# Layer 2's 3x3 convolution: neighbour columns stacked by ScalarE copies instead of DMAs

## The chip, the cores and the metric

The kernel runs on one NeuronCore of a Trainium2 chip. The metric is the device time of one execution in microseconds (us). The engines are TensorE (PE, with its weight loads PEld), VectorE (DVE), ScalarE (ACT), GpSimd (POOL) and SyncE (SP). DMAs are issued from the queues of SP, POOL and ACT. Each engine works through its own instructions in the order of the program and waits where an operand is not ready or a buffer is not free.

## The reference

Four layers of the form x = x + layer(GN(x)) on x of shape (1024, 16, 16, 16): batch, height h, width w, channels. GN is a group normalisation without weights, 8 groups of two channels. Layer 0 is a tensor-train matrix product, layers 1 and 3 are two steps of a cellular automaton, and layer 2, which the change is about, is a plain convolution:

```python
def _L2_conv_ref(x, filters, bias):
    out = jax.lax.conv_general_dilated(x, filters, window_strides=(1, 1), padding='SAME',
        dimension_numbers=('NHWC', 'HWIO', 'NHWC'))
    return out + bias
...
x = x + _L2_conv_ref(_gn(x), L2_conv_filters, L2_conv_bias)   # filters (3, 3, 16, 16)
```

## The kernel before

The batch is cut into two halves of 512 images, n = 0 and 1. One half of x is held in SBUF at a time for the layer that works (`X0` or `X1`, each 128 partitions x 32 lines x 512 floats, 8 MB), while the other buffer is loaded from DRAM and normalised for the stage that follows. All is float32. Between layers x lies in DRAM (`xf`).

In layer 2 a line holds one image row h and one half of its columns (wh = 0: columns 0 to 7, wh = 1: columns 8 to 15). Its 128 partitions are 4 column pairs x 16 channels x 2 columns of a pair. So a matmul with a 128x128 weight (`fw`, one for each of the three rows of the filter) does all of the filter inside one half of the columns: `inner(h, y)`. What crosses the middle is left: the rightmost column of the left half needs column 8 and the leftmost of the right half needs column 7. `across(h)` adds this with one matmul a half into 32 of the 128 output partitions. Its moving operand is `hx`: for one row h the 16 channels of the neighbour column in the three rows h-1, h, h+1, stacked in 48 partitions (from 0 for wh = 0, from 64 for wh = 1). `halo(k)` fetches it for four rows at a time with DMAs from SBUF to SBUF on SP's queue (`L1153`, `L1156`), three for each half, one more each at the top edge.

Two rows h and h+1 make a group of steps: `first(h)`, `inner(h, 1)`, `first(h+1)`, `inner(h+1, 1)`, then `across` of both, then `last(h)`, `last(h+1)`. Six PSUM banks hold the accumulators `po` of three rows, two for each row. `finish(h)` empties the two banks of row h with ScalarE (bias added, into `r`, six buffers, `L1191`) and adds the result to x in DRAM with an accumulating DMA on GpSimd's queue (`L1192`). `finish` of an even row stands in `last(h)`, that of an odd row in `first` of the next row.

`run(layer, us, loads, (background, lo, hi), by)` weaves three things into one program: the main steps of the layer, the loads of the other half (issued evenly over the first `by` of the steps), and the background steps (the normalisation of the half being loaded), placed by their costs between the fractions `lo` and `hi` of the steps. The normalisation sums the lines on DVE (`s1`, `L589` and `L592`), takes the mean with a matmul (`pmean`), copies it to SBUF on ScalarE (`m`, `L636`), subtracts it (`L621`), squares the lines on ScalarE (`sq`, `L606`) and adds the squares on DVE (`L592`, `s2s` at `L596`), takes the variance with a matmul (`pvar`), and multiplies by the inverse root. In the first half of layer 2 the other half is normalised whole (`norm_lines`, line layout); in the second in four quarters (`norm_cw`, for layer 3's layout, in which spread matmuls `pr` follow). In the second half the loads read what the first half has just accumulated in DRAM. `line_sum(..., own=True)` forms the sum of squares: one step makes the square of the next two lines and adds it. `t4` is the buffer of squares and partial sums, three of them in these stages. `hx` has three buffers.

Of the kernel before, what the change touches and what calls it, by code (L numbers as in the profile page):

```python
# [12 lines left out]
ALU = mybir.AluOpType  # L13
# [5 lines left out]
B, S, C = 1024, 16, 16  # L19
P = 128  # L20
NB = 512
# [82 lines left out]
def conv_preact_kernel(ctx: ExitStack, tc: tile.TileContext, a: dict, out: bass.AP):  # L104
# [55 lines left out]
    def cst(name, shape, dt=F32):  # L160
        return const.tile(shape, dt, tag=name, name=name)
# [245 lines left out]

    b2 = cst("b2", [P, 1])

    convw = cst("convw", [P, 448])  # L410

    def conv_weights():


        room = work([P, 2, NB], "t4", "convn").rearrange("p a b -> p (a b)")
        fn = room[:, 0:384].rearrange("p (y w o) -> p y w o", y=3, w=8)
        hn = room[:, 384:400]
        fw = convw[:, 0:384].rearrange("p (y w o v) -> p y w o v", y=3, w=4, v=2)
        hw = convw[:, 384:448].rearrange("p (e o v) -> p e o v", e=2, v=2)
        V.memset(room[:, 0:400], 0.0)  # L420
        V.memset(hw, 0.0)
        f = a["L2_conv_filters"]
        with nc.allow_non_contiguous_dma(reason="weights"):
            for w in range(8):
                for kw in range(3):
                    if 0 <= w + kw - 1 < 8:
                        wi = w + kw - 1
                        G.dma_start(
                            fn[32 * (wi // 2) + wi % 2 : 32 * (wi // 2) + 32 : 2, :, w],
                            f[:, kw].rearrange("y i o -> i y o"),  # L430
                        )
            for wh in range(2):
                for y in range(3):
                    r0 = 64 * wh + 16 * y
                    G.dma_start(hn[r0 : r0 + 16], f[y, 2 - 2 * wh])
            for m in range(4):
                for v in range(2):
                    G.dma_start(
                        b2[32 * m + v : 32 * m + 32 : 2], a["L2_conv_bias"].unsqueeze(1)
                    )  # L440

        def spread():
            for y in range(3):
                V.tensor_copy(fw[:, y], fn[:, y].rearrange("p (w v) o -> p w o v", v=2))
            for wh in range(2):
                rows = slice(64 * wh, 64 * wh + 64)
                for e in range(2):
                    V.tensor_copy(hw[rows, e, :, 1 - wh], hn[rows])
                V.memset(hw[64 * wh : 64 * wh + 16, 1], 0.0)

        return spread

# [125 lines left out]
    def line_sum(parts, name, own, dear=False):  # L578

        st = {}

        def first():
            if own:
                st["t"] = parts[0]()
                return add(parts[1])()
            st["t"] = work([P, 2, NB], "t4", name)
            V.tensor_tensor(st["t"], parts[0](), parts[1](), ALU.add)  # L589

        def add(p):
            return lambda: V.tensor_tensor(st["t"], st["t"], p(), ALU.add)  # L592

        def last():
            st["s"] = work([P, NB], "s", name + "s")
            V.tensor_tensor(st["s"], st["t"][:, 0], st["t"][:, 1], ALU.add)  # L596

        x = 1.2 if dear else 0.0
        return st, [(1.2 + 2 * x, first)] + [(1.2 + x, add(p)) for p in parts[2:]] + [(0.8, last)]

    def squares(X, l0, n, on_act):
        def piece(l):
# [367 lines left out]
    def layer_train():  # L970
# [160 lines left out]

    conv = dict(
        fw=convw[:, 0:384].rearrange("p (y m) -> p y m", y=3),
        hw=convw[:, 384:448].rearrange("p (e m) -> p e m", e=2),
    )

    def layer_conv(X, n):

        st = {}

        def start():
            halo(0)

        def halo(k):
            t = st["h", k] = work([P, 4, NB], "hx", "hx")
            for wh in range(2):
                src = X[slice(97, 128, 2) if wh else slice(0, 32, 2), 16 * (1 - wh) : 16 * (1 - wh) + 16]
                for y in range(3):  # L1150
                    r0, h0 = 64 * wh + 16 * y, 4 * k + y - 1
                    lo, hi = max(h0, 0), min(h0 + 4, S)
                    nc.sync.dma_start(t[r0 : r0 + 16, lo - h0 : hi - h0], src[:, lo:hi])  # L1153
                    if lo > h0:

                        nc.sync.dma_start(t[r0 : r0 + 16, 0:1], src[:, 0:1])  # L1156

        def inner(h, y):
            for wh in range(2):
                T.matmul(  # L1160
                    st["po", h][wh], conv["fw"][:, y], X[:, 16 * wh + h + y - 1],
                    start=y == max(0, 1 - h), stop=y == min(2, S - h),
                )

        def across(h):
            rows = 32 if h == S - 1 else 48
            for wh in range(2):
                cols = slice(0, 32) if wh else slice(96, 128)
                T.matmul(
                    st["po", h][wh][cols], conv["hw"][64 * wh : 64 * wh + rows, h == 0],  # L1170
                    st["h", h // 4][64 * wh : 64 * wh + rows, h % 4], start=False, stop=False,
                )

        def first(h):
            if h % 2 == 0 and h > 0:
                finish(h - 1)
            if h % 4 == 1 and h + 4 < S:
                halo(h // 4 + 1)
            st["po", h] = [bank([P, NB], "o", "po2") for _ in range(2)]
            inner(h, max(0, 1 - h))  # L1180

        def last(h):
            inner(h, min(2, S - h))
            if h % 2 == 0 or h == S - 1:
                finish(h)

        def finish(h):

            for wh in range(2):
                r = work([P, NB], "r", "conv")  # L1190
                A.activation(r, st["po", h][wh], AF.Identity, bias=b2)  # L1191
                G.dma_start(rows_wc(xf[2][n], wh, h), r.unsqueeze(1), accum_op=ALU.add)  # L1192

        steps = []
        for h in range(0, S, 2):
            for j in (h, h + 1):
                steps.append(lambda j=j: first(j))
                if 0 < j < S - 1:
                    steps.append(lambda j=j: inner(j, 1))
            steps += [  # L1200
                lambda h=h: (across(h), across(h + 1)), lambda h=h: last(h), lambda h=h: last(h + 1)
            ]
        return start, steps

# [313 lines left out]
    last = alone(N, 3) + rstd(nst, slice(96, 128)) + [3] + scaled(N, [3])  # L1518
    nca_sb = dict(t4=2, s=3, n=2, wq=5, mask=1, f=5, hid=8, u=2, r=4, nx=1)
    nca_ps = dict(h=6, o=2)  # L1520
    conv_sb, conv_ps = dict(gn, s=3, r=6, hx=3), dict(o=6, m=2)
    on_vector[0] = True
    with ExitStack() as es:
        shared[0] = "o"
# [8 lines left out]
    with ExitStack() as es:  # L1533
        shared[0] = "m"
        stage(es, conv_sb, conv_ps)
        run(layer_conv(X0, 0), 108, load_wc(X1, xf[2][1]), (norm_lines(X1), 0.09, 1.1), by=0.12)
        run(
            layer_conv(X1, 1), 108, [put(L3)] + load_cw(X0, xf[3][0]), (norm_cw(X0, True), 0.09, 1.04), by=0.12
        )
    with ExitStack() as es:  # L1540
        shared[0] = "o"
# [41 lines left out]
```

## Time and profile before

Median 3199.57 us of three runs (3197.21 to 3203.37). The profiled execution spans 3190.1 us.

| engine | busy us | share of the span |
|---|---|---|
| PE | 3058.5 | 96% |
| DVE | 1785.6 | 56% |
| ACT | 1018.3 | 32% |
| POOL | 670.6 | 21% |

Layer 2 takes the window from 2339.7 to 2591.5 us. In it the groups that matter here are (instructions are records; a float32 matmul leaves two):

| line | engine | what | count | busy us | mean ns |
|---|---|---|---|---|---|
| L1160 | PE | inner matmuls, 128x128 weights | 368 | 168.5 | 609 |
| L1169 | PE | crossing matmuls, 48 (32) x 32 weights | 128 | 35.8 | 646 |
| L1191 | ACT | evictions | 64 | 42.6 | 685 |
| L606 | ACT | squares of two lines | 32 | 32.7 | 1052 |
| L621 | DVE | subtract the mean, multiply | 62 | 72.2 | 1165 |
| L1192 | POOL | accumulating DMAs issued | 64 | 55.5 | 949 |

How to read a profile line of a group: line, engine, operation, out<-in by the program's names, shape and count; then busy time and mean; then the engine's idle time just before these instructions and what ended it. Two matmuls can overlap, so a mean longer than the spacing is usual. "PEclk" is the clock that TensorE was granted, in tenths.

### The profile page before, as it was taken

Reading aid. Unit: us, or ns where it says so; the run is one execution under the profiler, and the core shown is the slowest. Engines: PE = TensorE matmul, PEld = TensorE weight load, DVE = VectorE, ACT = ScalarE, POOL = GpSimd, SP = SyncE. Lnnn points to the kernel's source line nnn. Section 1 sums busy time; section 2 is a strip of 40 time slices with the busy share of each in tenths; the row PEclk is TensorE's granted clock in tenths of the full one; section 3 lists DMA queues with packets and bytes.
Section 4 is the critical chain, followed back from the end, with each engine's and each line's share of the span. In section 5 each row is a group of like instructions: output and inputs, shape, how many; then the busy total and the mean of one; then the engine's idle time right before and its main releaser. Section 6 shows DMA issues by size and latency. Waiting matters only on the chain.

```text
span 3190.1 us, 37179 instructions
## 1 busy us (share of the span) xinstructions
PE 3058.5 (96%) x13874; PEld 1260.3 (40%) x13874; DVE 1785.6 (56%) x2378; ACT 1018.3 (32%) x1690; POOL 670.6 (21%) x706
## 2 busy tenths in 40 slices
PE   7899899999999999999999999999979899999996
PEld 5444333444444444444444433333323233333332
DVE  5255345755554555544556678558757647754222
ACT  4331221100001000000111166666624356655553
POOL 1116532200000000000000034435432124432221
PEclk8999999999999999999999999999989999999998
DMA  7535545443333433322222254454476765433445
GB/s 283 201 142 97 121 101 160 133 144 104 104 109 132 146 116 104 104 98 96 90 95 90 76 168 133 129 167 154 139 192 110 185 139 173 136 92 115 128 137 186
DMA packets 243299, 424.77 MB, mean 133 GB/s; under 512 B 37844, under 2 KB 91952, under 8 KB 239408
## 3 DMA queue, kind: packets, MB, share of 16 engines
q1 hardware_dynamic: 217824, 368.63, 35.5%
q0 software_dynamic: 24480, 53.48, 8.3%
q8 instruction: 110, 1.80, 0.2%
q14 instruction: 69, 0.57, 0.1%
q10 hardware_dynamic: 816, 0.30, 0.0%
HBM read 238.78 MB, written 165.60 MB: 127 GB/s over the span
## 4 chain that ended last, share of the span: by engine, by line
issue 46%; PE 31%; POOL 8%; DMA 4%; DVE 2%; SPq 1%; ACT 1%; POOLq 0%; DVEq 0%; ACTq 0%
PE ph L1410 11%; PE po L1078 10%; PE po L1263 4%; POOL res L1313 4%; POOL u L1312 4%; PE po L1160 2%; DMA xn<-xf 1%; PE L_conv_pe L382 1%; SPq L941 1%; DVE xn L621 1%; DMA hx<-xn 1%; PE pw L1001 1%; PE ptout L948 1%; DVE sq L592 1%; POOL L_conv_wy L394 0%
## 5 line engine op out<-in xcount | busy, mean ns | idle before, releaser
L1078 PE MATMUL po<-xn,w 128*128 128x512 f32 x3584 | 1584.3, 598 | 4.6 <-DVE xn L892 4.6
L1078 PEld LDWEIGHTS po<-xn,w 128*128 128x128 f32 x3584 | 669.9, 190 | 852.6 <-issue 833.7
L1413 ACT ACTIVATE hid<-ph,pack 128x512 f32<-128x512 f32 x1024 | 653.9, 686 | 429.2 <-PE ph L1410 308.4
L1114 DVE TENSOR_TENSOR r<-r,po 128x512 f32<-128x512 f32 x576 | 377.8, 683 | 499.0 <-PE po L1078 476.3
L1312 POOL TENSOR_TENSOR u<-u,mask 128x512 f32<-128x512 f32 x128 | 202.5, 1582 | 1858.9 <-DMA nx<-xn 1241.7
L1410 PE MATMUL ph<-xn,wq 32*128 32x512 f32 x3664 | 573.1, 613 | 1.5 <-DMA wq<-L_conv_wy 1.5
L1006 ACT COPY w<-pw 128x512 f32<-128x512 f32 (+1 forms) x320 | 150.6, 558 | 1194.0 <-issue 970.4
L1410 PEld LDWEIGHTS ph<-xn,wq 32*128 32x128 f32 x3664 | 228.6, 184 | 263.3 <-issue 231.4
L1410 PE MATMUL ph<-xn,pack 32*128 32x512 f32 x1288 | 302.2, 631 | 4.5 <-ACT hid L1413 3.2
L1263 PE MATMUL po<-hid,pack 128*32 128x512 f32 x2048 | 283.0, 609 | 1.2 <-DVE u L1275 0.9
L1019 DVE TENSOR_TENSOR w<-w 128x512 f32<-128x512 f32 x320 | 211.2, 684 | 115.2 <-ACT w L1006 114.7
L621 DVE TENSOR_TENSOR xn<-xn,m 128x1024 f32<-128x1024 f32 x160 | 225.9, 1461 | 47.1 <-ACT m L636 47.1
L1313 POOL TENSOR_TENSOR res<-res,u 128x512 f32<-128x512 f32 x128 | 215.2, 1681 | 17.0 <-PE po L1263 2.7
L1275 DVE SCALAR_TENSOR_TENSOR u<-po,pack,xn 128x512 f32<-128x512 f32 x128 | 95.9, 749 | 157.6 <-PE po L1263 150.9
L1160 PE MATMUL po<-xn,convw 128*128 128x512 f32 x368 | 168.5, 609 | 0.0
L1410 PEld LDWEIGHTS ph<-xn,pack 32*128 32x128 f32 x1288 | 114.5, 187 | 100.7 <-issue 61.7
L1114 DVE TENSOR_TENSOR xn<-xn,po 128x512 f32<-128x512 f32 x96 | 64.3, 684 | 125.9 <-PE po L1078 125.8
L592 DVE TENSOR_TENSOR sq<-sq 128x1024 f32<-128x1024 f32 x78 | 110.6, 1418 | 15.2 <-ACT sq L606 12.0
L1263 PEld LDWEIGHTS po<-hid,pack 128*32 128x32 f32 x2048 | 42.9, 108 | 189.7 <-issue 137.4
L394 POOL DMA_DIRECT2D L_conv_wy<-xn x160 | 89.0, 563 | 99.0 <-ACT xn L152 90.7
L1160 PEld LDWEIGHTS po<-xn,convw 128*128 128x128 f32 x368 | 69.3, 193 | 99.3 <-issue 96.7
L592 DVE TENSOR_TENSOR s<-s,xn 128x1024 f32<-128x1024 f32 x60 | 86.4, 1441 | 29.1 <-DMA xn<-xf 27.9
(163 smaller groups left out, 1776.9 us busy)
## 6 DMA issues: line engine op xcount, KB each, us to landing
xf<-r SPq DMA_DIRECT2D x112, 512.0 KB, 3.8
xn<-xf SPq DMA_DIRECT2D x96, 512.0 KB, 5.1
r<-xf SPq DMA_DIRECT2D x80, 512.0 KB, 4.5
wq<-L_conv_wy SPq DMA_DIRECT2D x192, 192.0 KB, 2.8
res<-xf SPq DMA_DIRECT2D x128, 256.0 KB, 3.0
xf<-res SPq DMA_DIRECT2D x96, 256.0 KB, 2.0
res<-xr SPq DMA_DIRECT2D x256, 64.0 KB, 2.8
xf<-conv POOLq DMA_DIRECT2D x64, 256.0 KB, 6.1
```

Of the source, the lines that this page charges most:

```text
L592: return lambda: V.tensor_tensor(st["t"], st["t"], p(), ALU.add)
L621: V.tensor_tensor(part, part, m().unsqueeze(1).broadcast_to([P, 2, NB]), op)
L1006: A.copy(w[:, k0:4, :, 32 * r : 32 * r + 32].rearrange("p k t (v o) -> p v (k t) o", v=2), pw[r],)
L1019: V.tensor_tensor(w[:, k], w[:, x], w[:, y], ALU.add if sign > 0 else ALU.subtract)
L1078: T.matmul(po, st["w", u][:, matrix, t], x, start=t == 0, stop=t == 3)
L1114: V.tensor_tensor(r[at], r[at], po, ALU.add if sign > 0 else ALU.subtract)
L1160: T.matmul(st["po", h][wh], conv["fw"][:, y], X[:, 16 * wh + h + y - 1], start=y == max(0, 1 - h), stop=y == min(2, S - h),)
L1263: T.matmul(po[32 * j : 32 * j + 32], nca["w1"][:, v], hid[j], start=v == 0, stop=v == 1)
L1312: G.tensor_tensor(u, u, st["m"][:, w2], ALU.mult)
L1313: G.tensor_tensor(r, r, u, ALU.add)
L1410: T.matmul(ph, w, x, start=k == 0, stop=k == len(tiles) - 1)
L1413: A.activation(h, ph, AF.Relu, bias=nca["bt"][:, r : r + 1])
```

## The change

The DMAs of `halo` become ScalarE copies. [...] the stack is laid out anew. The neighbour column lies in 16 of 32 partitions (every second one); all 32 are copied, and zero rows of the weight take out the 16 that are not wanted. Four blocks of 32 partitions hold lines 4k-1+b and 4k+1+b for b = 0 to 3, so a pair of rows h, h+1 finds the four lines h-1 to h+2 in the four blocks at once, and the weight (`hw`, now one for each wh and each parity e of the row) picks three of them. A crossing matmul has 128 rows (96 in the last pair) instead of 48. The eight copies of the first stack run at the start; those of the next are put into `pending` and taken out one at each main step. GpSimd zeroes the line above the image once.

Beside this: `finish` of a row stands one or two steps later in the program, and its DMA is put into `waiting` and issued later again, so that the loads come first; `r` gets 12 buffers for that. The loads are issued over the first 0.07 of the steps instead of 0.12. `put(L3)`, a weight load for layer 3, comes after the loads. The squares are made one step ahead of the add that uses them. The spans of the background end at 1.04 and 1.06 instead of 1.1 and 1.04.

```diff
-    convw = cst("convw", [P, 448])
+    convw = cst("convw", [P, 512])
...
-                    r0 = 64 * wh + 16 * y
-                    G.dma_start(hn[r0 : r0 + 16], f[y, 2 - 2 * wh])
+                    for e in range(2):
+                        r0 = 32 * (y + e)
+                        G.dma_start(hn[r0 + wh : r0 + 32 : 2, wh, e], f[y, 2 - 2 * wh])
...
         def first():
             if own:
-                st["t"] = parts[0]()
-                return add(parts[1])()
+                st["t"], st["q"] = parts[0](), parts[1]()
+                return add(1)()
...
-        def add(p):
-            return lambda: V.tensor_tensor(st["t"], st["t"], p(), ALU.add)
+        def add(i):
+            def go():
+                x = st["q"] if own else parts[i]()
+                if own and not dear and i + 1 < len(parts):
+
+                    st["q"] = parts[i + 1]()
+                V.tensor_tensor(st["t"], st["t"], x, ALU.add)
+                if own and dear and i + 1 < len(parts):
+                    st["q"] = parts[i + 1]()
+
+            return go
...
         def start():
-            halo(0)
+            for copy in halo(0):
+                copy()
...
-                for y in range(3):
-                    r0, h0 = 64 * wh + 16 * y, 4 * k + y - 1
-                    lo, hi = max(h0, 0), min(h0 + 4, S)
-                    nc.sync.dma_start(t[r0 : r0 + 16, lo - h0 : hi - h0], src[:, lo:hi])
...
+            def begin():
+                st["h", k] = work([P, 2, 2, NB], "hx", "hx")
+                if k == 0:
+                    G.memset(st["h", k][0:32, :, 0], 0.0)
+
+            def copy(b, wh):
+                ls = [l for l in (4 * k - 1 + b, 4 * k + 1 + b) if 0 <= l < S]
+                at = (ls[0] - (4 * k - 1 + b)) // 2
+                l0 = 16 * (1 - wh) + ls[0]
+                A.copy(
+                    st["h", k][32 * b : 32 * b + 32, wh, at : at + len(ls)],
+                    X[96 * wh : 96 * wh + 32, l0 : l0 + 2 * len(ls) - 1 : 2],
+                )
...
+            rows = slice(0, 96 if h >= S - 2 else P)
             for wh in range(2):
                 cols = slice(0, 32) if wh else slice(96, 128)
                 T.matmul(
-                    st["po", h][wh][cols], conv["hw"][64 * wh : 64 * wh + rows, h == 0],
-                    st["h", h // 4][64 * wh : 64 * wh + rows, h % 4], start=False, stop=False,
+                    st["po", h][wh][cols], conv["hw"][rows, wh, h % 2],
+                    st["h", h // 4][rows, wh, h // 2 % 2], start=False, stop=False,
                 )
...
         def first(h):
+            if h % 4 == 0 and h + 4 < S:
+                pending.extend(halo(h // 4 + 1))
+            st["po", h] = [bank([P, NB], "o", "po2") for _ in range(2)]
+            inner(h, max(0, 1 - h))
+            if h % 2 == 0 and h > 0:
+                finish(h - 2)
+
+        def middle(h):
+            inner(h, 1)
             if h % 2 == 0 and h > 0:
                 finish(h - 1)
...
         def last(h):
             inner(h, min(2, S - h))
-            if h % 2 == 0 or h == S - 1:
+            if h == S - 1:
+                finish(h - 1)
                 finish(h)
+
+        def step(*fs):
+            def go():
+                for f in fs:
+                    f()
+                if pending:
+                    pending.pop(0)()
...
                 A.activation(r, st["po", h][wh], AF.Identity, bias=b2)
-                G.dma_start(rows_wc(xf[2][n], wh, h), r.unsqueeze(1), accum_op=ALU.add)
+                waiting.append((rows_wc(xf[2][n], wh, h), r.unsqueeze(1)))
+            while waiting and 2 * h + 2 - len(waiting) < 4 * (h - 4):
+                G.dma_start(*waiting.pop(0), accum_op=ALU.add)
...
-    conv_sb, conv_ps = dict(gn, s=3, r=6, hx=3), dict(o=6, m=2)
+    conv_sb, conv_ps = dict(gn, s=3, r=12, hx=3), dict(o=6, m=2)
...
-        run(layer_conv(X0, 0), 108, load_wc(X1, xf[2][1]), (norm_lines(X1), 0.09, 1.1), by=0.12)
+        run(layer_conv(X0, 0), 108, load_wc(X1, xf[2][1]), (norm_lines(X1), 0.09, 1.04), by=0.07)
         run(
-            layer_conv(X1, 1), 108, [put(L3)] + load_cw(X0, xf[3][0]), (norm_cw(X0, True), 0.09, 1.04), by=0.12
+            layer_conv(X1, 1), 108, load_cw(X0, xf[3][0]) + [put(L3)], (norm_cw(X0, True), 0.09, 1.06), by=0.07
         )
```

## The prediction

> **What bounds the kernel now.** I read the page first. TensorE is busy for 96% of the span, so only its idle time and its slow-clock time can be won. The slices show two dips, near slices 29 and 31 (about 80 us each).
>
> ```profile
> PE   7899899999999999999999999999979899999996
> ...
> PEclk8999999999999999999999999999989999999998
> ```
>
> Both lie in layer 2, from the first convolution matmul at 2339.7 us to the last at 2591.5: 251.8 us. The change's code acts there, apart from the order of squares and adds in the other norms. Second view: what PE waited for in that window (total, times, longest).
>
> ```profile
> PE pmean L675 <- DVE s1s L596: 12.4, 1, 12.4
> PE pmean L704 <- DVE s1s L596: 11.0, 1, 11.0
> PE po L1169 <- DMA hx<-xn: 6.2, 2, 5.4
> PE pvar L708 <- DVE s2s L596: 4.9, 2, 2.6
> PE pvar L679 <- DVE s2s L596: 0.6, 1, 0.6
> ```
>
> That is 35.1 us of idle PE: 19.2 in the first half (X0; it ends near 2464) and 15.9 in the second. Most of it is not the convolution's own work: PE takes its instructions in order, and the mean and variance matmuls of the *next* normalisation stand among the convolution's, waiting for sums over lines that are still being loaded. Third view: PE in order of time, start, length, instructions.
>
> ```profile
> 2350.50 1.88 PE L1169 MATMUL po<-hx,convw 48*32 48x512 f32 x2 [5.39 <-DMA hx<-xn]
> 2353.19 3.59 PE L1169 MATMUL po<-hx,convw 48*32 48x512 f32 x6 [0.81 <-DMA hx<-xn]
> 2356.71 12.39 PE L1160 MATMUL po<-xn,convw 128*128 128x512 f32 x24
> ...
> 2370.88 10.57 PE L1160 MATMUL po<-xn,convw 128*128 128x512 f32 x24
> 2393.86 2.08 PE L675 MATMUL pmean<-s1s,gm_wc 128*128 128x512 f32 x2 [12.41 <-DVE s1s L596]
> ...
> 2421.56 1.91 PE L1169 MATMUL po<-hx,convw 48*32 48x512 f32 x8
> ```
>
> 24 records cost 10.57 us, but 12.39 after the first wait, and 8 crossing records 1.91 or up to 5.5: a wait is paid twice, the second time in clock. Undisturbed, two rows of the image take 10.57 + 1.84 = 12.4 us, one half 96 us (8 pairs less two edge steps), so both halves need 192, plus 14 for the 14 mean, variance and spread matmuls (about 1 us each). 252 - 206 = 46 us: 35 idle and 11 of slow clock. That is the most that can be won.
>
> Why are the sums late? Fourth view, the DMA queues from 2360 to 2393.
>
> ```profile
> q1 hardware_dynamic: 2056, 7.57, 71.8%
> q0 software_dynamic: 1152, 2.10, 34.4%
> ```
>
> q1 carries loads and halo pieces, q0 the accumulating evictions; together they fill all 16 engines. Loads queue behind eight halo issues at 2344.9 to 2349.9 and six more at 2351.5 to 2355.5. The last sum ends at 2393.8 (2391.78 + 1.22 + 0.69). In the second half the loads cannot start before the last eviction of X0 has landed (2470.5), and two loads later six halo issues again take 2471.5 to 2475.6.
>
> Fifth view: ScalarE in the same window, which the change loads.
>
> ```profile
> L1191 ACT ACTIVATE conv<-po,b 128x512 f32<-128x512 f32 x63 | 41.9, 685 | 123.4 <-PE po L1160 123.2
> L606 ACT ACTIVATE sq<-xn 128x1024 f32<-128x1024 f32 x32 | 32.7, 1052 | 10.6 <-DVE sq L592 7.8 <-DVE xn L621 2.7
> ```
>
> ScalarE works 78 of 252 us.
>
> **What the Trainium skill says.** "TensorE: Matmul & The Clock Gate", Part 1, has the array throttled to half clock after an idle window of about 3.4 us; the trace agrees: the 5.39 us wait is followed by slow matmuls, while the two pvar waits (4.9 us together, 2.6 the longest) are not: there 4 records still take 1.98 us. The same page, Architectural detail, calls ScalarE and VectorE strictly first in, first out, so a copy delays the eviction behind it. "DMA: Bandwidth & Descriptors", Issuing engines are not separate DMA queues, has all queues share the same 16 engines; the 71.8% and 34.4% above agree. "TensorEngine Tiling (Array Packing)", Tiling Modes, lists four 128x32 column tiles.
>
> **The change part by part.**
>
> *Halo DMAs removed.* 52 issues of 0.5 to 1.4 us leave SyncE. Loads of the first half start near 2345 instead of 2349.9, and the 4th at once instead of at 2355.6. From 2360 to 2393 q1 took 0.718 x 33 = 23.7 us for 7.57 MB (319 GB/s); 8.4 MB of loads then need 26 us, or 22 at the 387 GB/s that the window 2490 to 2500 shows. The eight evictions of these 33 us took 0.344 x 33 = 11.4 us of the engines. 2345 + 2 + (22 to 26) + (0 to 11.4) = 2369 to 2384, the sum 2 us later: PE's mean matmul at 2381 to 2386, not 2393.9. I take 2384: 10 us won, and 2 of clock, since a wait under 3 us leaves it up. by=0.07 adds little: the queue, not the program order, held them.
>
> *Evictions some steps late.* GpSimd waits only for ScalarE's results, and nothing stands between the evictions on its queue. A DMA written later in the program is issued there at the same moment. I cost the delayed DMA at nothing. What does move is the ScalarE ACTIVATE, now one or two steps behind PE: ScalarE no longer sits in an ACTIVATE waiting for PE while squares queue behind it. With squares one step ahead this removes most DVE waits on squares (9.4 us), and with them the 4.9 of pvar; I leave 1.
>
> *ScalarE copies.* Per half 32 copies, 28 of 1024 and 4 of 512 elements a partition. Nearest row: a square of 1024, 1.052 us alone, 0.98 in a run of three; "ScalarE: Activation LUTs", What ACT_TABLE_LOAD costs, prices 186 + 0.833 x 1024 = 1039 ns. I take 0.97 and 0.56: 29.4 us a half, ends 0.9 and 1.1. Mostly beside PE, but in three places on its path:
> - Start of half one. All eight must end before the first crossing matmul: 6 x 0.97 + 2 x 0.56 = 6.9 us. ScalarE is free at 2338.7, but hx lies in memory that the stage before gives back, whose last reader is GpSimd (mask at 2343.1, res at 2344.4), and the memset follows there (1.0 us, from 514 ns for 512). Start 2338.7 to 2344.4: wait 1 to 7.4 us against 6.2 now. I take no gain; the loads set the next wait anyway.
> - Start of half two. The copies queue behind the last evictions: 1.4 + 6.9 = 8.3 us after the half begins; PE wants them at 5.3. +3.2 us where there was nothing.
> - The squares of half one. Placing the background steps by the kernel's rule, 13 squares, 7 copies and 2 rows' evictions stand between row 6's eviction and the end of row 8's: 13.0 + 6.8 + 4.1 = 24 us. Row 11 needs row 8's two banks (six banks are three rows) after 9 x 1.76 + 1.84 = 17.7 us. +6 us of PE, and 2 of clock. In half two the squares come in fours and I find no such queue.
>
> *Crossing matmuls.* As many, with 128 rows instead of 48, two column tiles at once instead of two row tiles: column tiles do overlap (8 records of L1263, 128*32, take 1.00 to 1.12 us with four tiles). Two at once give 1.8 us, as now: 0, ends -0.3 and +0.5 a step.
>
> *Half two's mean.* Loads from about 7 us after the half begins, no halo between: four loads of 2.1 MB end 7.5 us later, the sum at 16.5; PE comes at 5.3 + 3.2 + 1.8 + 5 x 1.76 = 19. The 11.0 us vanish, with 3.3 of clock (2.08 + 3.62 + 2.19 against 4.6).
>
> *The rest.* Weight DMAs and copies lie in layer 0's slack; the swap of squares and adds where VectorE squares has the same operations; put(L3) later meets no reader.
>
> Sum: half one -10 - 2 + 6 + 2 = -4; half two -11 - 3.3 - 4 + 3.2 = -15. 3199.6 - 19 = 3181 us.
>
> **The rivals.**
> - *All waits go* (3165): copies start at 2339 or the late evictions do leave the loads alone, and the bank wait stays under 1 us: 34.4 removed, none back. For it: ScalarE's 78 of 252 us. Against: strict order on ScalarE, and GpSimd's own queue.
> - *Loads stay the limit in half one* (3189): evictions share the engines as now, and the mean moves by 2, not 10. For it: full DMA slices. Against: 14 halo issues less ahead.
> - *Half of the copies show* (3196 to 3200, no change): 30 of 59 us on PE's path against 34 removed. For it: the six banks. Against: only 23 of 64 copies stand where PE is near.
> - *ScalarE becomes the bound* (slower, 3226): no copy is hidden, 59 - 33. For it: copies, squares and evictions in one ordered queue. Against: ScalarE would hold 137 of some 240 us.
>
> **How the numbers follow.** 0.45 for 3181, 0.22 for 3165, 0.13 for 3189, 0.10 for no change, 0.10 for slower. The first three are faster: 0.80. The range 3163 to 3197 holds all but the slower case, half of the no-change case, and a little under 3163.
>
> **What would show it.** Right: layer 2 spans about 233 us; pmean waits of at most 3 us; a PE wait on ScalarE near the squares of half one (row 11), and one of about 3 us at the first crossing of half two; copies near 0.97 us; the first eviction DMAs issued as soon as row 0 is evicted, long before row 5; the crossing groups still near 1.9 us. Wrong: copies over 1.2 us, pvar waits that grow, or a pmean wait of 8 us and more that names a DMA as its source.

## The result, and the profile after

The changed kernel takes 3166.84 us in the median (3157.47 to 3175.82), beside 3198.39 us for the kernel before on the same chip: a ratio of 0.9898 [0.9867, 0.9929]. The forecast of 3181 us had the right sign, and its range held the time, but the gain was under-estimated: 19 us were forecast, 31.6 measured, and 28.4 in the repeat that opens the experiments.

The profiled span fell from 3190.1 to 3163.8 us. The page's slices show the two dips of layer 2 filled: slice 29 (counted from 0) in the rows of PE and of its clock, and slice 31 in that of PE, where the clock had shown no dip:

```profile
PE   7899899999999999999999999999999999999996
...
PEclk8999999999999999999999999999999999999997
```

From its first convolution matmul (2336.2 us) to the first matmul of the next layer (2560.1), layer 2 takes 223.9 us instead of 251.8: 27.9 us less. Half one takes 112.4 instead of 124.3, half two 111.5 instead of 127.5 (half two starts inside a merged line, at 2448.6 after and 2464.0 before). The spans differ by 26.3 us, so layer 2 holds all of the gain; the part before it is 3.5 us shorter and the part after it 5.1 us longer. These two parts aren't quite constant: in the profiles of this study layer 2 begins between 2336.2 and 2344.7 us, and what follows it takes 597.7 to 603.7, in no order that the edits explain. The experiments are therefore read from the length of layer 2 first, and from the ratio second.

What PE waited for in layer 2 (total, times, longest, in us), after:

```profile
PE po L1190 <- ACT hx L1169: 6.9, 2, 4.7
PE po L1181 <- ACT conv L1229: 5.1, 1, 5.1
PE pvar L716 <- DVE s2s L604: 1.3, 1, 1.3
```

35.1 us became 13.3. Both waits of the mean matmuls are gone, and of the variance's 5.5 us 1.3 are left. Two new waits name ScalarE: the stacks (`hx`), and two banks that an eviction (`conv`) had not yet emptied. PE in order of time (start, length, engine, line, tile, records, and in brackets the wait):

```profile
2346.26 4.41 PE L1190 MATMUL po<-hx,convw 128*32 128x512 f32 x8 [4.68 <-ACT hx L1169]
...
2373.34 1.02 PE L683 MATMUL pmean<-s1s,gm_wc 128*128 128x512 f32 x2
2374.29 1.91 PE L1190 MATMUL po<-hx,convw 128*32 128x512 f32 x8
...
2413.02 6.46 PE L1181 MATMUL po<-xn,convw 128*128 128x512 f32 x8 [5.08 <-ACT conv L1229]
...
2456.10 4.10 PE L1190 MATMUL po<-hx,convw 128*32 128x512 f32 x8 [2.18 <-ACT hx L1169]
2460.13 8.85 PE L1181 MATMUL po<-xn,convw 128*128 128x512 f32 x20
2468.82 1.02 PE L712 MATMUL pmean<-s1s,gm_cw 128*128 128x512 f32 x2
```

A mean matmul without a bracket and with 1.02 us for its two records (2.08 before) comes at 2373.3, which is 37.2 us after the layer's start, where it was 54.2 before. The lengths again carry the second half of each wait: eight crossing records take 1.91 us undisturbed but 4.41 and 4.10 after a wait, and eight inner records 6.46 where 3.5 is usual (10.57 for 24).

Why the sum is early enough: DVE's adds of the loaded lines, each of which waits for its 512 KB,

```profile
2347.76 8.91 DVE L596 TENSOR_TENSOR s<-s,xn 128x1024 f32<-128x1024 f32 x7
...
2362.35 1.23 DVE L596 TENSOR_TENSOR s<-s,xn 128x1024 f32<-128x1024 f32 x1 [1.34 <-DMA xn<-xf]
2364.94 1.23 DVE L596 TENSOR_TENSOR s<-s,xn 128x1024 f32<-128x1024 f32 x1 [1.37 <-DMA xn<-xf]
...
2370.13 1.22 DVE L596 TENSOR_TENSOR s<-s,xn 128x1024 f32<-128x1024 f32 x1 [1.35 <-DMA xn<-xf]
2371.39 0.69 DVE L604 TENSOR_TENSOR s1s<-s 128x512 f32<-128x512 f32 x1
```

come 1.27 us apart at first (8.91 / 7) and 2.6 us apart later (2362.35 to 2364.94). The DMA queues of the two stretches, 2341 to 2355 and then 2355 to 2371 (packets, MB, share of the 16 engines), tell why:

```profile
q1 hardware_dynamic: 1486, 5.17, 96.5%
```

```profile
q1 hardware_dynamic: 962, 3.48, 56.6%
q0 software_dynamic: 813, 1.50, 51.1%
```

Until 2355 the loads have the engines almost alone (one last store of 256 KB is among the 5.17 MB) and bring more than half of their 8.4 MB; then the accumulating evictions of q0 come, 1.5 MB, and take half of the engines. The sum ends at 2372.1 (2371.39 + 0.69), only 1.3 us before PE comes to the mean. GpSimd in order of time shows when they are issued:

```profile
2337.49 2.07 POOL L1353 TENSOR_TENSOR u<-u,mask 128x512 f32<-128x512 f32 x1 [1.82 <-DVE u L1316]
...
2340.84 0.94 POOL L1163 MEMSET hx<- 32x1024 f32 x1
2354.54 1.84 POOL L1232 DMA_DIRECT2D xf<-conv  x2 [12.76 <-ACT conv L1229]
2356.88 1.72 POOL L1232 DMA_DIRECT2D xf<-conv  x2 [0.50 <-ACT conv L1229]
```

The code issues row 0's DMA behind the eviction of row 5, which ScalarE makes at 2379.9, but on the chip it goes out 25 us before that, as soon as ScalarE has written its result. And ScalarE, whose copies are the price of all this:

```profile
2339.59 13.93 ACT L1169 COPY hx<-xn 32x512 f32<-32x512 f32 x14 [4.46 <-POOL u L1353]
...
2408.67 2.00 ACT L614 ACTIVATE sq<-xn 128x1024 f32<-128x1024 f32 x2
2410.69 0.61 ACT L1169 COPY hx<-xn 32x512 f32<-32x512 f32 x1
2411.33 1.06 ACT L614 ACTIVATE sq<-xn 128x1024 f32<-128x1024 f32 x1
2412.30 1.25 ACT L1229 ACTIVATE conv<-po,b 128x512 f32<-128x512 f32 x2
```

The first stack waits for the mask step of the stage before on GpSimd (2337.49 + 2.07), whose memory it takes over. At 2408 to 2412 squares and copies stand ahead of the eviction, and PE, whose last matmul ended at 2407.9 (2400.81 + 7.13), waits for that eviction until 2413.0. ScalarE's copies by shape (count, busy us, mean ns, idle):

```profile
L1169 ACT COPY hx<-xn 32x1024 f32<-32x1024 f32 x56 | 58.3, 1041 | 0.9
L1169 ACT COPY hx<-xn 32x512 f32<-32x512 f32 x8 | 4.9, 614 | 4.6 <-POOL u L1353 4.5
```

63.2 us of new ScalarE work. It is idle for long enough elsewhere that only 12 us of PE's waits (6.9 + 5.1) name it as what they waited for.

### The profile page after: what moved, and what is told of

Same layout as the page of the kernel before. It is cut to its first block, busy times and chain, and to the rows that moved or that the text cites. A ratio compares the mean times of both kernels' runs of the same rounds, so it can differ in the third digit from the quotient of the medians.

```text
span 3163.8 us, 37175 instructions
## 1 busy us (share of the span) xinstructions
PE 3054.8 (97%) x13874; PEld 1258.0 (40%) x13874; DVE 1783.3 (56%) x2374; ACT 1080.6 (34%) x1754; POOL 673.2 (21%) x714
## 4 chain that ended last, share of the span: by engine, by line
issue 49%; PE 30%; POOL 9%; DMA 3%; SPq 1%; DVE 1%; POOLq 0%; ACT 0%; DVEq 0%; ACTq 0%
PE ph L1451 11%; PE po L1086 9%; PE po L1304 4%; POOL u L1353 3%; POOL res L1354 3%; PE po L1181 2%; PE L_conv_pe L382 1%; POOL xf L1232 1%; DMA L_conv_wy<-xn 1%; SPq L949 1%; PE ptout L956 1%; PE pw L1009 1%; POOL L_conv_wy L394 0%; PE ptx L1363 0%; DMA xn<-xf 0%
```

## The experiments

Every kernel below is the changed kernel with the edit shown, unless it says otherwise. "Layer 2" is measured as above. Ratios are to the kernel before, run beside it.

| run | ratio [95%] | layer 2, us |
|---|---|---|
| after_again | 0.9908 [0.9894, 0.9923] | 227.2 |
| dma_halo | 0.9975 [0.9965, 0.9985] | 245.7 |
| no_lag | 0.9906 [0.9890, 0.9923] | 223.2 |
| old_order | 0.9915 [0.9895, 0.9935] | 226.2 |
| stack_only | 0.9962 [0.9950, 0.9974] | 242.1 |
| old_finish | 0.9939 [0.9923, 0.9955] | 234.5 |
| old_squares | 0.9906 [0.9889, 0.9922] | 224.0 |
| opt_bank | 0.9878 [0.9864, 0.9892] | 216.5 |
| opt_all | 0.9928 [0.9915, 0.9941] | 229.7 |
| all_gate | 0.9863 [0.9846, 0.9879] | 212.2 |
| bank_gate | 0.9888 [0.9873, 0.9904] | 215.3 |
| dma_halo_act | 1.0044 [1.0028, 1.0060] | 262.5 |

My theory was that the stack is the bulk (it takes the halo issues out of the loads' way), that the late ACTIVATEs keep ScalarE's queue open, and that the deferred DMA does nothing. The rivals: the gain is the new order of loads and evictions, and the stack itself is a wash; or the stack alone does it all.

### The changed kernel again

> The changed kernel once more, for its spread. Its four times so far lie between 3157 and 3176 us. My theory: layer 2 is the same in every execution, 224 to 226 us from its first convolution matmul to the next layer's first matmul (before: 251.8), with PE waits of about 4.7 us (first stack), 5.1 us (row 11) and 2.2 us (stack of the second half); the spread of some 9 us each way lies in other layers. Rival: the spread is one of these waits, then the waits differ by several us between the two profiles.

3166.18 us (3163.30 to 3168.96) against 3194.56. The same three waits, with the variance's at 2.9 instead of 1.3 us; 227.2 us of layer 2 lie above the 224 to 226 that I expected. So 223.9 and 227.2 are two readings of one program, and a difference of 3 us in layer 2 needs more than one profile behind it.

### Everything but the stack: dma_halo

The halo is fetched by the DMAs of the kernel before, in the old layout; order, evictions, squares and spans stay as changed.

```diff
-            if h % 4 == 0 and h + 4 < S:
-                pending.extend(halo(h // 4 + 1))
+            if h % 4 == 1 and h + 4 < S:
+                halo(h // 4 + 1)
...
+                    nc.sync.dma_start(t[r0 : r0 + 16, lo - h0 : hi - h0], src[:, lo:hi])
```

> All of the change but the ScalarE stack: the neighbour lines come by the 26 DMAs a half of before, in the old layout. My theory (the halo DMAs stood ahead of the loads and filled the DMA engines): the mean wait of the first half comes back with 5 to 10 us and that of the second with 2 to 8; the waits of 5.1 (row 11) and 2.2 us are gone; layer 2 takes 230 to 237 us, 3172 to 3180 us in all. Rival (the gain is the order of loads, evictions and squares): no mean wait, layer 2 about 215 us, 3157 us.

Layer 2 took 245.7 us: 21.8 more than changed, so the direction was right and the size larger than I expected. What PE waited for in layer 2, SyncE's DMA issues in order of time, and one of DVE's adds in half two:

```profile
PE pmean L684 <- DVE s1s L605: 12.3, 1, 12.3
PE pvar L717 <- DVE s2s L605: 8.8, 1, 8.8
PE po L1179 <- DMA hx<-xn: 6.2, 2, 5.4
PE pmean L713 <- DVE s1s L605: 2.1, 1, 2.1
PE po L1170 <- ACT conv L1218: 0.5, 1, 0.5
```

```profile
2347.17 2.50 SPq L775 DMA_DIRECT2D xn<-xf  x5
2349.77 4.89 SPq L1163 DMA_DIRECT2D hx<-xn  x6
2355.43 9.12 SPq L775 DMA_DIRECT2D xn<-xf  x9
```

```profile
2487.85 1.23 DVE L589 TENSOR_TENSOR s<-xn 128x1024 f32<-128x1024 f32 x1 [8.31 <-DMA xn<-xf]
```

The half's first mean wait is back at 12.3 us, to 0.1 us what it was before the change (12.4). The loads start 10 us after the layer's start (2337.0), and after five of them six halo issues hold the queue for another 5.7 us. Issuing the loads earlier *in the program* can't help while halo DMAs stand ahead of them on the same queue. The variance wait of 8.8 us in half two is a late load too: DVE stands 8.31 us for it, with the subtraction and the squares behind. And without copies on ScalarE the bank wait is 0.5 us.

### The halo DMAs on another queue: dma_halo_act

As dma_halo, with the halo DMAs on ScalarE's queue, so that SyncE's queue carries loads alone.

```diff
-                    nc.sync.dma_start(t[r0 : r0 + 16, lo - h0 : hi - h0], src[:, lo:hi])
+                    nc.scalar.dma_start(t[r0 : r0 + 16, lo - h0 : hi - h0], src[:, lo:hi])
```

> The run with the halo DMAs, these now issued from ScalarE's queue instead of SyncE's. It tells apart in which way the halo DMAs hold the loads: by standing ahead of them on SyncE, or by taking the DMA engines. If the queue order counts (as my prediction had it): the loads start near 5 us after the layer's start instead of 10, and the mean wait of the first half, 12.3 us with SyncE, falls to 5 us or less; layer 2 by 5 us or more under the 245.7 of that run. If the engines count: the wait stays at 9 us or more.

The loads start early (2343.6), and no mean wait is left. But the whole is 262.5 us and slower than the kernel before, where I expected a gain over dma_halo. What PE waited for:

```profile
PE po L1179 <- DMA hx<-xn: 42.5, 4, 17.1
PE po L1170 <- ACT conv L1218: 4.0, 1, 4.0
```

The wait has moved from the mean to the crossing matmuls. The eight issues of the first stack, which SyncE had done from 2342.2 to 2347.1, now stretch from 2341.8 to 2359.2, with gaps of more than 5 us after the third and the sixth (what holds ScalarE's queue there isn't shown), and in half one each piece lands 2.3 to 8.8 us after its issue, beside the 512 KB loads. The Trainium skill, "DMA: Bandwidth & Descriptors", Issuing engines are not separate DMA queues, says that DMAs of all issuing engines run on the same 16 engines and interleave; this run agrees, at the price of 42.5 us.

PE reached the mean only at 2394.4, because it had waited 21 us for the halo first, so that the mean no longer waits doesn't by itself show that the sum was early. DVE's end of the sum does, here and in dma_halo:

```profile
2379.86 0.69 DVE L605 TENSOR_TENSOR s1s<-s 128x512 f32<-128x512 f32 x1
```

```profile
2390.51 0.69 DVE L605 TENSOR_TENSOR s1s<-s 128x512 f32<-128x512 f32 x1
```

From the layer's start (2338.4 here) the sum takes 42.1 us, in dma_halo 54.2, in the changed kernel 35.9. So it is 12 us earlier than in dma_halo, where the loads stood behind halo DMAs, and 6 later than with the copies. But the first evictions also left some 15 us later here, as PE had waited, and so kept out of the loads' way: how much of the 12 us is the queue's order alone stays open. Taking the halo off the DMA engines, not onto another queue, is what the copies do.

### The stack alone: stack_only

The kernel before with the ScalarE copies and nothing else: the edits of old_finish, no_lag, old_squares and old_order below, all at once.

```diff
-        run(layer_conv(X0, 0), 108, load_wc(X1, xf[2][1]), (norm_lines(X1), 0.09, 1.04), by=0.07)
+        run(layer_conv(X0, 0), 108, load_wc(X1, xf[2][1]), (norm_lines(X1), 0.09, 1.1), by=0.12)
...
+            if h % 2 == 0 and h > 0:
+                finish(h - 1)
...
+            if h % 2 == 0 or h == S - 1:
+                finish(h)
```

> The kernel before with the ScalarE stack as its only change: evictions, squares, loads, spans and six buffers r as before. My theory (the 26 DMAs a half were the cost, the rest moves little): no mean wait of more than 2 us; the row 11 wait is gone, since an even row is emptied one step earlier and fewer squares stand ahead of it; variance waits of 3 to 8 us in the second half, as the squares stand behind evictions that wait for PE; layer 2 219 to 228 us, 3160 to 3172 us in all. Rival (late evictions and squares one step ahead are needed beside the stack): layer 2 above 232 us.

242.1 us: the expectation of 219 to 228 missed, and the rival, by which the copies need room on ScalarE, was right. What PE waited for:

```profile
PE pvar L707 <- DVE s2s L595: 11.2, 3, 6.2
PE po L1181 <- ACT hx L1160: 6.9, 2, 4.7
PE pvar L678 <- DVE s2s L595: 4.5, 1, 4.5
```

Both mean waits are gone, so that the stack alone removes them is shown. But 15.7 us of variance waits take their place, where the kernel before had 5.5 and the changed one has 1.3.

### Evictions at their old places: old_finish

Everything as changed, except that ScalarE's ACTIVATE of a row stands right behind the row's matmuls again (the two places of `finish` in the diff above).

> The changed kernel with the evictions at their old places in the program, one or two steps earlier. My theory: the row 11 wait of 5.1 us and its 2.9 us of slow clock go, variance waits grow by 2 to 5 us; layer 2 218 to 224 us. Rival (ScalarE blocked by evictions that wait for PE costs more): variance waits of 8 us and more, layer 2 above 228 us.

234.5 us; the expectation of 218 to 224 missed. PE waits 14.5 us for variances, and 0.8 instead of 5.1 for banks. The waits of ScalarE and DVE in layer 2 say why, first with the evictions at their old places, then in the changed kernel:

```profile
ACT conv L1226 <- PE po L1181: 61.5, 32, 10.1
...
DVE sq L596 <- ACT sq L614: 16.1, 10, 5.1
```

```profile
ACT conv L1229 <- PE po L1181: 36.7, 29, 8.6
...
DVE sq L596 <- ACT sq L614: 8.2, 10, 1.7
```

An ACTIVATE that stands right behind its matmuls in the program holds ScalarE until PE is there, 61.5 us in all. Squares and copies queue behind it, DVE's sum of squares waits twice as long for them, and the variance matmul waits for DVE. One or two steps later the ACTIVATE finds its bank finished more often: ScalarE stands still for 25 us less, and layer 2 is 10.6 us shorter. The price is the bank wait.

### The smaller parts: no_lag, old_order, old_squares

The eviction's DMA directly behind its ACTIVATE, with the old six buffers:

```diff
-            while waiting and 2 * h + 2 - len(waiting) < 4 * (h - 4):
+            while waiting:
...
-    conv_sb, conv_ps = dict(gn, s=3, r=12, hx=3), dict(o=6, m=2)
+    conv_sb, conv_ps = dict(gn, s=3, r=6, hx=3), dict(o=6, m=2)
```

> The changed kernel with each accumulating DMA written right behind its eviction and six buffers r again. My theory: GpSimd issues a DMA when ScalarE has made its operand, wherever it stands in the program, so nothing changes: layer 2 224 to 226 us, the first issue about 1 us after the first eviction, the time within 0.2% of the changed kernel. Rival (late DMAs leave the engines to the loads, or six buffers make ScalarE wait): the last load of the first half lands 3 us or more later and a mean wait or an eviction's wait for a DMA appears.

223.2 us, just under the 224 to 226 expected, with the same three waits. The deferral and its six extra buffers do nothing, because GpSimd has no other work in its queue between the evictions: an instruction's later place in the program is a later time only where something stands in between.

The loads over 0.12 of the steps, the weights first, the background's ends at 1.1 and 1.04 (the lines of `run` as before the change):

> The changed kernel with the loads spread over 0.12 of the steps, put(L3) ahead of the loads and the background spans 1.1 and 1.04 as before. My theory (the queue ahead of the loads, not their place in the program, held them): no mean wait in the first half; in the second at most 2 us more for the 416 KB ahead of the loads; the row 11 wait falls by about 3 us, as three squares less stand ahead of row 8's eviction; layer 2 222 to 228 us. Rival (loads first is what counts): mean waits of 5 us or more.

226.2 us, within what two profiles of the changed kernel differ by. One wait moved as expected: the bank wait is 2.6 instead of 5.1 us, since the background is spread wider and 10 squares instead of 13 stand between row 6's eviction and row 8's.

The square of two lines in the step that adds it, as before the change:

```diff
-                x = st["q"] if own else parts[i]()
-                if own and not dear and i + 1 < len(parts):
-
-                    st["q"] = parts[i + 1]()
-                V.tensor_tensor(st["t"], st["t"], x, ALU.add)
+            return lambda: V.tensor_tensor(st["t"], st["t"], p(), ALU.add)
```

> The changed kernel with each square made in the step of its own add again, evictions and all else as changed. My theory (a square can only be late where it stands behind an eviction, and the late evictions have cured that): variance waits grow by 3 to 6 us, the row 11 wait falls by 1 (one square less stands ahead), layer 2 226 to 232 us. Rival (one step ahead is what keeps VectorE fed): variance waits of 8 us and more, layer 2 above 234 us.

224.0 us; I had expected 226 to 232. No effect can be measured: with the ACTIVATEs late, the squares are early enough anyway.

### Removing the bank wait: opt_bank

In half one all stacks are copied before the squares begin (a fourth `hx` buffer, paid by four of the `r` buffers that the no_lag run showed to be idle):

```diff
-            if h % 4 == 0 and h + 4 < S:
+            if n == 0 and h == 0:
+                pending.extend(halo(1) + halo(2))
+            elif n == 0 and h == 4:
+                pending.extend(halo(3))
+            elif n == 1 and h % 4 == 0 and h + 4 < S:
                 pending.extend(halo(h // 4 + 1))
...
-    conv_sb, conv_ps = dict(gn, s=3, r=12, hx=3), dict(o=6, m=2)
+    conv_sb, conv_ps = dict(gn, s=3, r=8, hx=4), dict(o=6, m=2)
```

> The changed kernel with four buffers hx, so that in the first half all stacks are copied before the squares begin, with eight buffers r and each DMA right behind its eviction. My theory (copies among the squares hold row 8's eviction): the row 11 wait of 5.1 us falls to under 1, its slow clock of 2.9 us goes, layer 2 215 to 218 us. Rival (squares and evictions alone fill ScalarE there): the wait stays above 3 us.

216.5 us and 3155.18 us in all (3154.42 to 3161.96): as expected. The bank wait is 0.5 us. So taking the copies from between the squares is enough to let the eviction through; the squares alone still stand there. Both fill the queue, as the shorter wait with three squares less (old_order) shows.

### Removing the stack waits too: opt_all, and why it lost

Three edits: opt_bank; an eviction buffer taken before the first stack, so that the stack no longer lies where GpSimd's mask was; and half two's first stack copied during the last steps of half one.

```diff
         def start():
+            if n == 0:
+                spare.append(work([P, NB], "r", "conv"))
...
-        run(layer_conv(X0, 0), 108, load_wc(X1, xf[2][1]), (norm_lines(X1), 0.09, 1.04), by=0.07)
+        run(c0[:2], 108, load_wc(X1, xf[2][1]), (norm_lines(X1), 0.09, 1.04), (c1[2](0), 0.93, 0.97), by=0.07)
```

> As the run before it, with two more edits: in the first half one buffer r is taken before hx, so that hx lies in memory that no late reader of the layer before holds; and the first stack of the second half is copied in the last steps of the first. My theory: the waits of 4.7, 5.1 and 2.2 us all fall to under 1.5 us, with the slow clock after them; layer 2 204 to 210 us, 3145 to 3152 us in all. Rival (the loads then set the mean matmul of the first half): the start gained returns as a mean wait of 3 us or more, layer 2 210 us or more.

229.7 us instead of 204 to 210: the stack waits of 6.9 us are gone (0.3 left), and the whole is 13 us longer than opt_bank, as the rival had it. By halves, opt_bank took 104.9 and 111.5 us and opt_all 110.7 and 119.0, so both halves lost. What PE waited for, GpSimd's first eviction DMAs, and DVE's last add of a line in half one:

```profile
PE pmean L683 <- DVE s1s L604: 9.4, 1, 9.4
PE pvar L716 <- DVE s2s L604: 6.3, 1, 6.3
PE pmean L712 <- DVE s1s L604: 2.4, 1, 2.4
```

```profile
2350.01 1.84 POOL L1240 DMA_DIRECT2D xf<-conv  x2 [8.19 <-ACT conv L1237]
```

```profile
2374.80 1.23 DVE L596 TENSOR_TENSOR s<-s,xn 128x1024 f32<-128x1024 f32 x1 [1.37 <-DMA xn<-xf]
```

With no wait at its start PE is 4.4 us further on, the first eviction leaves at 2350.0 instead of 2354.5, and from 2356.6 on DVE's adds of the loads stand 2.6 us apart. The last lands 4.7 us later than in the changed kernel, while PE wants it earlier. In half two, where the first stack is early as well, PE comes sooner to sums whose loads can't start sooner, and the 2.4 and 6.3 us of waits follow. That PE's early wait had been protecting the loads is so far an argument.

### A gate for the evictions: all_gate and bank_gate

To test that, one GpSimd copy of a single column of the last line to be loaded, ahead of each half's first accumulating DMA. GpSimd's queue, and with it every eviction DMA, then stands still until the loads are in.

```diff
+    gate = cst("gate", [P, 1])
...
         def finish(h):
+            if h == 0:
+                G.tensor_copy(gate, XN[1 - n][:, NL - 1, 0:1])
```

all_gate is opt_all with the gate, bank_gate is opt_bank with it.

> The fourth kernel of the call before (all stacks early, hx off the mask's memory, the second half's first stack early) with one GpSimd instruction more ahead of the first accumulating DMA of each half: it copies one column of the last line being loaded, so that the evictions' DMAs really wait until the loads have landed. My theory (the first evictions, 4.5 us earlier there, share the DMA engines with the loads and set back the sums): the loads of the first half land 1.3 to 1.5 us apart to the end instead of 2.6, the mean wait of 9.4 us falls under 1.5, the variance wait of 6.3 in the second half under 3, layer 2 204 to 211 us, 3143 to 3152 us in all. Rival (the loads have their own pace of 2.6 us, or eight buffers r then stop ScalarE): mean wait above 5 us or PE waits on evictions.

> Early stacks in the first half and the gate that holds the first evictions' DMAs until the loads have landed, without the two edits for the first stacks. My theory (with the first stack late, the loads of the first half land in time anyway, 216.5 us of layer 2 without the gate): no change in the first half, the variance wait of 1.1 us in the second half no longer, layer 2 214 to 217 us, about 3154 us in all; so the gate pays only where the first stack is early. Rival (evictions and loads share the engines at a cost everywhere): layer 2 under 213 us.

all_gate: layer 2 in 212.2 us, 17.5 less than without the gate and 1 us over the expectation. DVE and GpSimd in order of time, in half one:

```profile
2349.57 16.57 DVE L597 TENSOR_TENSOR s<-s,xn 128x1024 f32<-128x1024 f32 x13 [0.63 <-DMA xn<-xf]
```

```profile
2364.85 0.18 POOL L1236 COPY gate<-xn 128x1 f32<-128x1 f32 x1 [23.08 <-DMA xn<-xf]
2365.38 8.86 POOL L1242 DMA_DIRECT2D xf<-conv  x10 [0.34 <-issue]
```

Thirteen adds stand 1.27 us apart to the end, the last load is in at 2364.9 instead of 2374.8, and ten eviction DMAs then leave in one go. No mean wait of half one is left. That loads and accumulating evictions compete, and that the order decides which of them PE feels, is shown. Half one takes 99.0 us, half two 113.2, where 2.9 us for a variance and 1.1 for a mean are left: the early stack of half two gains nothing that shows beside opt_bank's 111.5, even with the gate. 3152.49 us (3148.49 to 3155.19), 0.9863 [0.9846, 0.9879], is the lowest median of the study, but its interval overlaps opt_bank's, so that it beats opt_bank isn't shown.

bank_gate: 215.3 us, in its expected 214 to 217, and no gain that can be told from opt_bank's 216.5. Where PE still waits for its first stack, the loads win the race without help.

## Why the prediction was right, and where its size was off

The forecast reckons in the times of the kernel before. In the changed kernel layer 2 begins 3.5 us earlier, so 3.5 us are added to its times here before they are compared.

**The mean waits** (forecast: the mean matmul at 2384, 10 + 2 us won; measured: all 12.4, and 2.1 of clock, since the mean's two records and the next crossing group took 2.08 and 2.94 us before and 1.02 and 1.91 after). The cause was right: the halo DMAs (dma_halo 12.3 us, stack_only none); that it was their place ahead of the loads, and not also their share of the engines, isn't separated (dma_halo_act). The start of the loads was right too: near 2345, measured 2341.3 + 3.5. The mis-sized term was their end. I gave 2369 to 2384, and a mean matmul at 2384 puts it at 2382, near the top, with most of the evictions' 11.4 us of engine time added; the last add began at 2370.1 + 3.5 = 2373.6. More than half of the 8.4 MB were in before the first eviction could compete. opt_all and all_gate show the same end moved by 10 us by that competition.

**Start of half one** (forecast 0). The copies began at 2339.6 + 3.5 = 2343.1, inside the 2338.7 to 2344.4 that I gave: the reader that held them was the mask step, not the later `res`. PE's wait fell from 6.2 to 4.7 us, and the slow matmuls behind it from about 5.4 us of excess to 2.5: 4.4 us won. I had put it at nothing because the loads would set the next wait anyway; they didn't, for the sum ended 1.3 us before PE came to the mean. With the mean's 2.5 (14.5 - 12) this makes 6.9 of the 7.9 us by which half one was better than forecast (11.9 against 4).

**Bank wait of row 11** (forecast 6 + 2). Measured 5.1, and 6.46 - 3.5 = 2.9 of clock: right in cause (opt_bank) and in total. One term was wrong: two rows' evictions are four ACTIVATEs of 0.685 us, 2.7 and not 4.1, so the forecast should have had 22.5 us of ScalarE and a wait of 4.8. ScalarE took 22.3 us from the end of row 6's eviction to the end of row 8's.

**Start of half two** (forecast +3.2). 2.2 us of wait and 2.2 of slow clock. That the total of 4.4 is near is partly luck: the wait was shorter than forecast, and I had left out the clock, taking waits under 3 us as free.

**Half two's mean and the variances** (forecast: mean gone, 1 us of variance left). Measured: gone, and 1.3. Half two won 16.0 where 15 was forecast. But I credited the variance to the late ACTIVATEs and the early squares together. old_finish shows that it takes the ACTIVATEs, old_squares that the squares add nothing measurable to them, and dma_halo, with 8.8 us of variance wait in spite of both, that it takes early loads as well.

**Parts that I put at nothing**: the deferred DMAs (no_lag), the earlier loads (old_order) and the crossing matmuls' new shape (1.91 us for eight records in both kernels) moved nothing that could be measured. The copies took 1.041 us, not 0.97: nothing overlapped. The Trainium skill, "ScalarE: Activation LUTs", What ACT_TABLE_LOAD costs, would have been exact with its 186 + 0.833 x N, given there for an ACTIVATE: 1039 and 613 ns against 1041 and 614 measured.

So what was off is two terms of the sum, not a cause: the loads' end in half one, 8 us too late, and the gain at its start, put at nothing and worth 4.4. The rival of 3165 us came nearer in size, but by luck. Neither of its ways came true: the copies began 3.4 us into the layer and not at 2339, before it; the late evictions took half of the engines beside the loads; and the bank wait was 5.1 us, not under 1. It has 34.4 us of waits removed and none back; on balance 21.8 went (35.1 - 13.3).

**The parts don't add.** All but the stack wins 6.1 us of layer 2 (251.8 - 245.7), the stack alone 9.7, both together 27.9. Each half of the change leaves a wait that the other takes away: without the stack the loads are late (mean wait 12.3 us, variance wait 8.8), and with it alone ScalarE's queue is full in front of the squares (variance waits 15.7).

What stays open: why the times before and after layer 2 differ, by 3.5 and 5.1 us between the two kernels and by up to 8.5 and 6.0 us among all runs; and how the 12.3 us of dma_halo divide between the order on SyncE's queue and the load on the engines.

## What to carry to other kernels

Before moving a DMA, ask what stands ahead of it on its queue and what shares the engines with it: a place in the program changes nothing when the queue is empty between, and another queue only picks who waits. An instruction that waits at the head of an in-order queue costs what stands behind it, so put evictions where their operand is already finished, and copies where no eviction is due. A wait that is removed lets the next stage start sooner, and its transfers may then collide with ones that had been safe: here layer 2 grew from 216.5 to 229.7 us with two waits less, and fell to 212.2 once a gate kept the order.

## What the runs showed of the hardware that I had not expected

- Loads of 512 KB came 1.27 us apart alone (524288 bytes / 1.27 us = 413 GB/s at the least, since DVE's own adds take 1.23) and 2.6 us apart beside accumulating evictions: half the rate while 1.5 MB of evictions passed.
- A wait of 2.18 us was enough for slow matmuls (eight records in 4.10 instead of 1.91 us), while one of 2.62 us in the kernel before was not (two records in 1.04). The same 2.18 us at the same place were followed by 2.88 us in no_lag. So the length of a wait alone doesn't set its cost. The Trainium skill, "TensorE: Matmul & The Clock Gate", Part 1, has the clock fall after an idle window of about 3.4 us and calls this window free-running. The 2.18 us are shorter than the window, so here the measurement decides; that a wait's cost depends on where it falls would fit all three numbers, though no run tests it.
- A copy over 32 partitions costs what a square over 128 does: 1.041 us against 1.051 for 1024 elements a partition.
